# Last two images of a deformable convolution: the fine hats loaded to 32 partitions and copied on, and half of the first sums on another engine

## The chip, the cores and the metric

The kernel runs on one core of one Trainium2 chip. The metric is the device time of one execution in microseconds (us), over repeated executions. All data is float32.

## The reference, cut to what matters

Two layers are computed, one after the other, on 32 images of 128 channels and 32 x 32 pixels. Layer 0 is a sequence model (an encoder, a causal convolution of 64 taps per feature, a gated matmul, a layer norm, a decoder). Layer 1 is a deformable depthwise convolution of 8 x 8 taps, and the change lies there. For each tap `t` it reads the normalised image at a shifted position, by bilinear interpolation:

```
px = gx + koff_x[t] + off_x[t];   py = gy + koff_y[t] + off_y[t]
ix = px * W/(W-1) - 0.5;          iy = py * H/(H-1) - 0.5
s  = bilinear(image, iy, ix)      # zero outside
acc += s * weight[:, t]
out = x + gelu((acc - bn_mean) * inv + bn_beta)
```

The offsets of a tap are shared by all 128 channels, so `s` is a matrix product: a window of pixels (128 of them) by channels, against the interpolation weights of these pixels for each output pixel. The weight of a pixel at column `c`, row `r` is `hat(ix - c) * hat(iy - r)` with `hat(d) = max(0, 1 - |d|)`.

## The kernel before

`main_block` runs both layers in one stream. `first_part(b)` is the gated matmul, norm and decoder of image `b` in layer 0, and `second_part(b)` is the deformable convolution of image `b`. `run_along` interleaves the two by counting costs, `first_part(b + 2)` beside `second_part(b)`, so that the order of instructions on each engine is fixed when the kernel is built. For the last two images, 30 and 31, no `first_part` is left and `second_part` runs alone. While image 30 is worked on, the steps of `prepare(31)` are put in at given places: norm, offsets, and the hats of image 31.

The hats of an image lie in DRAM: `hats[0]` has 8 rows (the x hats, for 8 columns of a window) and `hats[1]` has 16 rows (the y hats, for its 16 rows). ScalarE makes them in `hat` (two instructions on 128 x 624 values) and stores them on its own DMA queue.

`second_part` goes over 17 packs of output columns, and in each over 4 pieces of two tap rows; so an image has 68 pieces, numbered `k` through all images. A full piece has 16 slots (output columns with one tap column each) of 2 x 32 values. For a piece:

- `load_hat(k, 0)` loads `s` (shown as `ds`) in 128 partitions: 16 copies of the 8 x hats. `load_hat(k, 1)` loads `hy` (`dhy`), each of the 16 y hats 8 times. A full piece has 512 KB of each. A pack at the left or right edge has several runs of slots and issues a DMA for each run. The loads go out on the queue of SyncE (SP). `s` has 5 buffers (`SB`) and `hy` 4 (`HB`): the load of `s` for piece `k + 5` is issued after the work of piece `k`.
- `weights(k)` (L989) multiplies `s` by `hy` on VectorE, two pieces ahead, just after the first product of the piece at hand; then it issues the load of `hy` four pieces further on.
- Three matmuls (L1032), one for each window of rows, multiply the window of pixels (`xw`, shown as `dxw`) by parts of `s` into PSUM (`dps`, 4 buffers). VectorE multiplies each result by the tap's weight into `prod` (`dp`, L1035, 3 buffers).
- GpSimd adds the two tap rows of `prod` (L1044), the first sum, and then adds the sum to `acc` (`dacc`, L1049), once for each output column of the pack.

At the end of an image GpSimd scales `acc` (L1055), ScalarE applies the gelu (L1059), VectorE adds the input (L1060), and the result is stored.

Other names: `spread` stores the positions of the taps to DRAM in 16 DMAs of 8 partitions each (`rel_d<-drel`), `gather` reads them back as `dr` (L888), `turn` transposes the image on PE and copies it to SBUF on ScalarE (`dtr`, L923), and `windows` loads `xw` (L1003). In `encode`, for layer 0, `u` (512 KB) is loaded for each image.

Of the kernel before, what the change touches and what calls it, by code (L numbers as in the profile page):

```python
# [15 lines left out]
B, C, H, W = 32, 128, 32, 32  # L16
# [430 lines left out]
NCOL = PIECES * NPIECE  # L447
# [13 lines left out]
def span_of(u):  # L461

    j0, j1 = max(0, 7 - u), min(7, NU - 1 - u) + 1
    return j0, j1 - j0


def rows_of(piece):

    a, b = 15 - KY2 * piece, 23 - KY2 * piece
    return (0, a), (a, b - a), (b, H - b)  # L470
# [30 lines left out]
def main_block(nc, tc, const, ins, x, u_d, y_d, x1_d, out, offmax):  # L501
# [15 lines left out]

    T = 512
    YB = 11
    SB, HB = 5, 4  # L520
    ctx = ExitStack()
    with ctx:

        def pool(name, bufs, space=None):
            kw = {} if space is None else {"space": space}
            return ctx.enter_context(tc.tile_pool(name=name, bufs=bufs, **kw))
# [3 lines left out]
        ppool = pool("mbp", 3)  # L530
        ypool = pool("mby", YB)
        tpool = pool("mbt", 5)
# [68 lines left out]
        for i in range(2):  # L601
            t = dram1.tile([2, NCOL], F32, tag=f"rel_d{i}", name=f"rel_d{i}")
            flat = t.rearrange("a (p l) -> (a p) l", p=P // 2)
            n = 2 * NCOL // P
# [5 lines left out]
        def at(t, offset, ap):  # L610
            return bass.AP(tensor=t.tensor, offset=t.offset + offset, ap=ap)
# [6 lines left out]
        def load(n, chunks):  # L618

            if n >= len(tiles):  # L620
                return
            b, hf = tiles[n]
            cols = slice(hf * T, hf * T + T)
            if n not in loaded:
                u = two.tile([P, T], F32, tag="gu", name=f"gu_{b}_{hf}")
                nc.sync.dma_start(u, u_d[b, :, cols])
                loaded[n] = u, []
            src = y_d[:, b].rearrange("d j l -> d (j l)")[:, cols]
            for k in chunks:
                y = ypool.tile([P, T], F32, tag="gy", name=f"gy_{b}_{hf}_{k}")  # L630
                nc.sync.dma_start(y, src[k * P : (k + 1) * P])
                loaded[n][1].append(y)
# [63 lines left out]
        def first_part(b, last=False):  # L696
            for hf in range(2):
# [5 lines left out]
                for m in range(KD):  # L703
# [13 lines left out]
                    if m == 1:  # L717
                        load(n + 1, range(YB - KD))
                        dec = pdec.tile([P, T], F32, tag="dec", name=f"gpo_{b}_{hf}")
# [9 lines left out]
                    for k in range(KD):  # L729
# [3 lines left out]
                        )  # L733
                        if m == KD - 1 and k < 2 * KD - YB:
                            load(n + 1, [YB - KD + k])
                        yield MM
# [210 lines left out]
        pieces = [(b, n, i) for b in range(B) for n in range(NP) for i in range(PIECES)]  # L947
        s_of, hy_of, xw_of = {}, {}, {}

        def slots_of(n):  # L950
            return sum(span_of(u)[1] for u in PACKS[n][1])

        def runs_of(n):

            runs, slot = [], 0
            for u in PACKS[n][1]:
                j0, nj = span_of(u)
                first = u * 8 + j0
                if runs and first == runs[-1][0] + runs[-1][2]:
                    runs[-1][2] += nj  # L960
                else:
                    runs.append([first, slot, nj])
                slot += nj
            return runs

        def load_hat(k, a):

            if k >= len(pieces):
                return
            b, n, i = pieces[k]  # L970
            hats = images[b][1]
            if a == 0:
                t = s_of[k] = spool.tile([P, 16, KY2, H], F32, tag="s", name=f"ds_{k}")
            else:
                t = hy_of[k] = hypool.tile([P, 16, KY2, H], F32, tag="hy", name=f"dhy_{k}")
            for first, slot, m in runs_of(n):
                dims = [[[0, 16], [NCOL, 8]], [[NCOL, 16], [0, 8]]][a]
                nc.sync.dma_start(
                    t[:, slot : slot + m],
                    at(hats[a], i * NPIECE + first * SLOT, [*dims, [1, m * SLOT]]),  # L980
                )

        def weights(k):

            if k >= len(pieces):
                return
            m = slots_of(pieces[k][1])
            s, hy = s_of[k], hy_of.pop(k)
            nc.vector.tensor_mul(s[:, :m], s[:, :m], hy[:, :m])  # L989
            load_hat(k + HB, 1)  # L990

        def windows(b, n):

            if n == NP:
                b, n = b + 1, 0
            x0 = PACKS[n][0]
            if b == B or (n > 0 and PACKS[n - 1][0] == x0):
                return
            t = xw_of[b, x0] = three.tile(
                [P, len(YWINDOWS), C], F32, tag="xw", name=f"dxw_{b}_{x0}"  # L1000
            )
            for j, y0 in enumerate(YWINDOWS):
                nc.sync.dma_start(  # L1003
                    t[:, j, :],
                    at(images[b][0], (y0 * W + x0) * C, [[W * C, 16], [C, 8], [1, C]]),
                )

        def second_part(b, steps):


            steps = sorted([*steps, *ending], key=lambda e: e[0])
            ending.clear()
            acc = one.tile([P, W, H], F32, tag="acc", name=f"dacc_{b}")
            nc.gpsimd.memset(acc, 0.0)
            for n in range(NP):
                x0, us = PACKS[n]
                m = slots_of(n)
                xw = xw_of[b, x0]
                windows(b, n + 1)
                for i in range(PIECES):  # L1020
                    k = (b * NP + n) * PIECES + i
                    s = s_of.pop(k)
                    w = wk[:, table_of[n] : table_of[n] + m, KY2 * i : KY2 * (i + 1)]
                    prod = ppool.tile([P, 16, KY2, H], F32, tag="prod", name=f"dp_{k}")
                    for j, (y0, ny) in enumerate(rows_of(i)):
                        while steps and steps[0][0] <= 3 * (PIECES * n + i) + j:
                            steps.pop(0)[1]()
                        ps = psam.tile([P, 512], F32, tag="sam", name=f"dps_{k}_{j}")
                        ps = ps[:, : m * KY2 * ny].rearrange(
                            "p (s k y) -> p s k y", s=m, k=KY2  # L1030
                        )
                        nc.tensor.matmul(  # L1032
                            ps, xw[:, j, :], s[:, :m, :, y0 : y0 + ny], start=True, stop=True
                        )
                        nc.vector.tensor_mul(  # L1035
                            prod[:, :m, :, y0 : y0 + ny],
                            ps,
                            w[:, :, :, None].to_broadcast([P, m, KY2, ny]),
                        )
                        if j == 0:  # L1040
                            weights(k + 2)
                        yield measure(m * KY2 * ny)
                    load_hat(k + SB, 0)
                    nc.gpsimd.tensor_add(prod[:, :m, 0], prod[:, :m, 0], prod[:, :m, 1])  # L1044
                    slot = 0
                    for u in us:
                        j0, nj = span_of(u)
                        to = acc[:, u - 7 + j0 : u - 7 + j0 + nj]
                        nc.gpsimd.tensor_add(to, to, prod[:, slot : slot + nj, 0])  # L1049
                        slot += nj  # L1050

            o = two.tile([P, L], F32, tag="img", name=f"do_{b}")
            xr = two.tile([P, L], F32, tag="img", name=f"dxr_{b}")
            nc.sync.dma_start(xr, x1_d[b])
            nc.gpsimd.tensor_scalar(  # L1055
                o.rearrange("p (h w) -> p w h", w=W), acc, bn_mean, bn_inv,
                op0=ALU.subtract, op1=ALU.mult,
            )
            ending.append((6, lambda: nc.scalar.activation(o, o, AF.Gelu, bias=bn_beta)))  # L1059
            ending.append((11, lambda: nc.vector.tensor_add(o, o, xr)))  # L1060
            ending.append((14, lambda: nc.scalar.dma_start(out[b], o)))

        ending = []
        def measure(columns):

            return columns + 40.0
# [24 lines left out]
        for b in range(B):  # L1091
            steps = prepare(b + 1) if b + 1 < B else []
            if b + 2 < B:
                run_along(
                    (first_part(b + 2, last=(b + 2 == B - 1)), FIRST),
                    (second_part(b, steps), SECOND),
                )
            else:
                run_along((second_part(b, steps), SECOND))
# [152 lines left out]
```

## Time and profile before

| | |
|---|---|
| time, median of 3 runs | 14067.17 us (14044.14 to 14073.55) |
| the profiled execution: its own time | 14059.14 us |
| its span, first to last instruction | 14057.0 us |
| PE busy (share of the span) | 13268.5 us (94%) |
| VectorE busy | 8827.7 us (63%) |
| GpSimd busy | 9113.7 us (65%) |
| ScalarE busy | 3215.1 us (23%) |
| moved by DMA | 3172.55 MB, mean 226 GB/s |

The engines are PE (matmul) and PEld (weight load) of TensorE, DVE (VectorE), ACT (ScalarE), POOL (GpSimd) and SP (SyncE). Shares of busy time are means over stages with different limits, so a change in one stage is read from stretches of the time line. Lines such as L989 are lines of the kernel before. A group of instructions is shown with its output and input by name and shape, its count, its busy time and mean, and the idle time of its engine just before it with what ended that.

### The profile page before, as it was taken

Reading aid. Unit: us, or ns where it says so; the run is one execution under the profiler, and the core shown is the slowest. Engines: PE = TensorE matmul, PEld = TensorE weight load, DVE = VectorE, ACT = ScalarE, POOL = GpSimd, SP = SyncE. Lnnn points to the kernel's source line nnn. Section 1 sums busy time; section 2 is a strip of 40 time slices with the busy share of each in tenths; the row PEclk is TensorE's granted clock in tenths of the full one; section 3 lists DMA queues with packets and bytes.
Section 4 is the critical chain, followed back from the end, with each engine's and each line's share of the span. In section 5 each row is a group of like instructions: output and inputs, shape, how many; then the busy total and the mean of one; then the engine's idle time right before and its main releaser. Section 6 shows DMA issues by size and latency. Waiting matters only on the chain.

```text
span 14057.0 us, 134776 instructions
## 1 busy us (share of the span) xinstructions
PE 13268.5 (94%) x40482; PEld 7317.0 (52%) x40482; DVE 8827.7 (63%) x12555; ACT 3215.1 (23%) x5422; POOL 9113.7 (65%) x9158
## 2 busy tenths in 40 slices
PE   5888889999999999999999999999999999999965
PEld 4777744555555555555555555555555555555532
DVE  6666614666666666666666666666666666666655
ACT  3445412222222222222222121222222222222210
POOL 1334413777777777777777777777777777777767
PEclk9999999999999999999999999999999999999977
DMA  6777724888888888888888888888888888889888
GB/s 224 232 232 230 222 79 126 239 237 235 233 231 232 231 233 238 236 235 230 231 232 229 229 229 230 229 234 237 239 236 233 230 233 231 233 236 237 233 228 227
DMA packets 1741840, 3172.55 MB, mean 226 GB/s; under 512 B 311218, under 2 KB 1030450, under 8 KB 1740082
## 3 DMA queue, kind: packets, MB, share of 16 engines
q1 hardware_dynamic: 1528498, 2708.63, 72.9%
q10 hardware_dynamic: 163456, 320.92, 6.4%
q0 software_dynamic: 49152, 134.28, 3.1%
q8 instruction: 329, 5.39, 0.2%
q14 instruction: 405, 3.32, 0.1%
HBM read 2697.07 MB, written 466.06 MB: 225 GB/s over the span
## 4 chain that ended last, share of the span: by engine, by line
PE 75%; DMA 10%; DVE 7%; POOL 3%; issue 2%; ACT 2%; SPq 1%; DVEq 0%; ACTq 0%; POOLq 0%
PE gpg L707 22%; PE gpv L730 21%; PE dps L1032 21%; DMA ds<-dhat 6%; PE psz L227 4%; PE gph L746 3%; PE gpo L639 3%; DVE dco L839 2%; DVE ds L989 2%; POOL y_d L296 1%; DMA y_d<-yo 1%; PE psy L266 1%; DVE dp L1035 1%; ACT t L280 1%; DMA dhy<-dhat 1%
## 5 line engine op out<-in xcount | busy, mean ns | idle before, releaser
L1032 PE MATMUL dps<-ds,dxw 128*128 128x256 f32 (+18 forms) x13056 | 4737.7, 450 | 308.0 <-DVE dp L1035 305.7
L1035 DVE TENSOR_TENSOR dp<-dps,k_weight_slots 128x256 f32<-128x256 f32 (+17 forms) x6528 | 3061.5, 485 | 2868.8 <-PE dps L1032 2578.2
L1049 POOL TENSOR_TENSOR dacc<-dacc,dp 128x256 f32<-128x256 f32 (+3 forms) x4736 | 4224.6, 892 | 371.4
L1044 POOL TENSOR_TENSOR dp<-dp 128x512 f32<-128x512 f32 (+3 forms) x2176 | 2858.6, 1314 | 2159.3 <-DVE dp L1035 2140.9
L1032 PEld LDWEIGHTS dps<-ds,dxw 128*128 128x128 f32 x13056 | 2478.6, 193 | 3330.7 <-issue 2510.7
L707 PE MATMUL gpg<-gy,g_w_glu 128*128 128x512 f32 x8192 | 3986.6, 593 | 19.1 <-DMA gy<-y_d 14.3
L730 PE MATMUL gpv<-gy,g_w_glu 128*128 128x512 f32 x8192 | 3975.3, 592 | 0.0
L989 DVE TENSOR_TENSOR ds<-ds,dhy 128x1024 f32<-128x1024 f32 (+3 forms) x2176 | 3158.0, 1451 | 1242.4 <-DMA ds<-dhat 1165.3
L707 PEld LDWEIGHTS gpg<-gy,g_w_glu 128*128 128x128 f32 x8192 | 1544.6, 190 | 1235.2 <-issue 974.2
L730 PEld LDWEIGHTS gpv<-gy,g_w_glu 128*128 128x128 f32 x8192 | 1548.9, 189 | 1158.2 <-issue 915.2
L767 ACT ACTIVATE gq<-gr 128x512 f32<-128x512 f32 x448 | 282.3, 630 | 5050.9 <-DVE gr L759 4725.9
L768 POOL TENSOR_TENSOR gs<-gs,gq 128x512 f32<-128x512 f32 x448 | 599.1, 1337 | 1267.2 <-ACT gq L767 1267.1
L266 PE MATMUL psy<-toe,z 128*128 128x192 f32 x4096 | 790.2, 353 | 222.9 <-DVE t L277 214.8
L266 PEld LDWEIGHTS psy<-toe,z 128*128 128x128 f32 x4096 | 735.5, 207 | 273.4 <-issue 211.1
L714 ACT ACTIVATE gs<-gpg,k_b_glu 128x512 f32<-128x512 f32 x512 | 351.8, 687 | 2151.3 <-PE gpg L707 2078.9
L903 ACT ACTIVATE dh<-dr,k_minus 128x624 f32<-128x624 f32 x768 | 620.5, 808 | 933.4 <-DMA dr<-rel_d 493.5
L296 POOL DMA_DIRECT2D y_d<-yo x1024 | 589.1, 583 | 351.8 <-ACT yo L290 324.2
L738 DVE SCALAR_TENSOR_TENSOR gs<-gpv,k_b_glu,gs 128x512 f32<-128x512 f32 x512 | 379.9, 742 | 413.8 <-PE gpv L730 413.8
L641 POOL TENSOR_TENSOR gs<-gs,gr 128x512 f32<-128x512 f32 x448 | 635.3, 1418 | 0.0
L904 ACT ACTIVATE dh<-dh,one 128x624 f32<-128x624 f32 x768 | 626.3, 815 | 25.0
L227 PE MATMUL psz<-w_enc,u 128*128 128x128 f32 x4096 | 584.5, 288 | 24.0 <-DVE z L234 9.1
L275 POOL MEMSET t<- 32x256 f32 x256 | 72.4, 322 | 776.0 <-ACT yo L290 775.1
(164 smaller groups left out, 6620.3 us busy)
## 6 DMA issues: line engine op xcount, KB each, us to landing
dhy<-dhat SPq DMA_DIRECT2D x1536, 512.0 KB
ds<-dhat SPq DMA_DIRECT2D x1536, 512.0 KB
dhat<-dh ACTq DMA_DIRECT2D x768, 312.0 KB
u<-u_d SPq DMA_DIRECT2D x256, 512.0 KB
y_d<-yo POOLq DMA_DIRECT2D x1024, 128.0 KB, 3.7
gy<-y_d SPq DMA_DIRECT2D x512, 256.0 KB
toe<-kp_d SPq DMA_DIRECT2D x128, 768.0 KB
dxw<-dvt_d SPq DMA_DIRECT2D x1248, 64.0 KB
```

Of the source, the lines that this page charges most:

```text
L227: nc.tensor.matmul(ps[:, j, :], u[:, (NB * g + j) * P : (NB * g + j + 1) * P], w_enc[:, k * P : (k + 1) * P], start=True, stop=True,)
L266: nc.tensor.matmul(ps[:, c // 2, c % 2, :], rows[i][:, g * CG + c0 + c, :], toe[:, c0 + c, :], start=True, stop=True,)
L296: nc.gpsimd.dma_start(y_d[d0 : d0 + CG, :, i * NB + j, :].rearrange("d b l -> b d l"), yo[i][j * B : (j + 1) * B],)
L641: nc.gpsimd.tensor_add(sums[0], sums[0], r)
L707: nc.tensor.matmul(gate, w_glu[:, k, D + m * P : D + m * P + P], ys[k], start=(k == 0), stop=(k == KD - 1),)
L730: nc.tensor.matmul(val, w_glu[:, k, m * P : m * P + P], ys[k], start=(k == 0), stop=(k == KD - 1),)
L904: nc.scalar.activation(t, t, AF.Relu, scale=-1.0, bias=const["one"])
L989: nc.vector.tensor_mul(s[:, :m], s[:, :m], hy[:, :m])
L1032: nc.tensor.matmul(ps, xw[:, j, :], s[:, :m, :, y0 : y0 + ny], start=True, stop=True)
L1035: nc.vector.tensor_mul(prod[:, :m, :, y0 : y0 + ny], ps, w[:, :, :, None].to_broadcast([P, m, KY2, ny]),)
L1044: nc.gpsimd.tensor_add(prod[:, :m, 0], prod[:, :m, 0], prod[:, :m, 1])
L1049: nc.gpsimd.tensor_add(to, to, prod[:, slot : slot + nj, 0])
```

## The change

For images 30 and 31 (`b >= ALONE`) the load of `s` brings 4 copies of the 8 x hats to 32 partitions, a quarter of the bytes. `spread_fine` then makes the other 96 partitions on ScalarE: partitions 0 to 31 are copied to 32 to 63, and 0 to 63 to 64 to 127. It is called one piece ahead of `weights`, just after it in program order. Of the first sums of these images, those of pieces with odd `i`, two of four, go to VectorE in place of GpSimd. The loads of `hy`, the matmuls and the number of DMAs are as before, and nothing changes for images 0 to 29 but three calls of `spread_fine` in the last three pieces of image 29.

```diff
+    ALONE = B - 2
...
+            rows = 4 if a == 0 and b >= ALONE else 16
             for first, slot, m in runs_of(n):
-                dims = [[[0, 16], [NCOL, 8]], [[NCOL, 16], [0, 8]]][a]
+                dims = [[[0, rows], [NCOL, 8]], [[NCOL, rows], [0, 8]]][a]
                 nc.sync.dma_start(
-                    t[:, slot : slot + m],
+                    t[: rows * 8, slot : slot + m],
                     at(hats[a], i * NPIECE + first * SLOT, [*dims, [1, m * SLOT]]),
                 )
+
+        def spread_fine(k):
+
+            if k >= len(pieces) or pieces[k][0] < ALONE:
+                return
+            m = slots_of(pieces[k][1])
+            for n in (32, 64):
+                nc.scalar.copy(s_of[k][n : 2 * n, :m], s_of[k][:n, :m])
...
                         if j == 0:
                             weights(k + 2)
+                            spread_fine(k + 3)
                         yield measure(m * KY2 * ny)
                     load_hat(k + SB, 0)
-                    nc.gpsimd.tensor_add(prod[:, :m, 0], prod[:, :m, 0], prod[:, :m, 1])
+                    adder = nc.vector if b >= ALONE and i % 2 else nc.gpsimd
+                    adder.tensor_add(prod[:, :m, 0], prod[:, :m, 0], prod[:, :m, 1])
```

## The prediction

> **What bounds the kernel now.** I read the span in equal slices first: PE is 90% busy or more in nearly all of it and falls to 60% only at the end. The timeline of GpSimd puts the clear of `acc` for image 30 at 13434 us and for image 31 at 13770 us, and the sum of image 31 ends at 14045 us. So the change acts on a tail of some 610 us, 136 pieces (2 images x 17 packs x 4). Busy time by stretch (us, PE, PEld, DVE, ACT, POOL, granted clock, DMA share, GB/s):
>
> ```profile
> 13000.00:13400.00 400.00, 398.37 (x1097) 205.12 (x1096) 261.24 (x358) 77.66 (x104) 287.00 (x268) 1.00 0.83 226
> ...
> 13825.00:13865.00 40.00, 23.50 (x59) 11.81 (x59) 25.62 (x39) 0.00 (x0) 33.02 (x31) 0.88 1.04 267
> ...
> 13945.00:13985.00 40.00, 23.20 (x54) 11.20 (x54) 23.87 (x39) 0.00 (x0) 30.78 (x27) 0.83 1.04 253
> ```
>
> Before the tail PE is full and DMA isn't. In it PE is 58% busy, ScalarE idle, GpSimd 80%, and the DMA engines are full (1.04). Groups of instructions from 13600 to 14000 us (busy, mean ns | idle before, releaser):
>
> ```profile
> L1049 POOL TENSOR_TENSOR dacc<-dacc,dp 128x256 f32<-128x256 f32 x142 | 139.1, 980 | 11.1
> ...
> L989 DVE TENSOR_TENSOR ds<-ds,dhy 128x1024 f32<-128x1024 f32 x70 | 97.0, 1386 | 136.9 <-DMA ds<-dhat 136.9
> L1044 POOL TENSOR_TENSOR dp<-dp 128x512 f32<-128x512 f32 x69 | 88.3, 1280 | 80.3 <-DVE dp L1035 80.3
> ```
>
> VectorE waits 137 us of 400 for the load of `ds`; PE waits for VectorE, and so does GpSimd. The chain of waits from 13800 us (start, length):
>
> ```profile
> 13800.56 10.59 DMA ds<-dhat
> 13811.15 0.02 issue
> 13811.17 0.04 DVE ds L989
> 13811.21 1.26 issue
> 13812.47 0.42 DVE dp L1035
> 13812.89 0.04 issue
> 13812.94 0.24 PE dps L1032
> 13813.18 9.66 DMA ds<-dhat
> ```
>
> A turn is 12.62 us: a load of `ds` is issued when PE has read the buffer, lands 10.6 us later, and is multiplied three pieces on. That is 4.21 us a piece. Weights counted from 13797 to 14000 us say the same: 46 full pieces and 4 half ones in 203 us, 4.23 us. A full piece loads 512 KB of `ds`, 512 KB of `dhy` and on average 48 KB of `dxw`; 68.6 kB on each of 16 engines in 4.23 us is 16.2 GB/s each. The queue is full, so the landing time is mostly queueing.
>
> [...] Stretches: image 31, 13900 to 13950 us; the encoder's loads of `u`, 205 to 245 us; and 13505 to 13545 us, with 16 stores of 8 partitions each.
>
> ```profile
> DMA packets 4100, 12.18 MB, mean 244 GB/s; under 512 B 455, under 2 KB 1228, under 8 KB 4097
> ...
> DMA packets 2498, 9.11 MB, mean 228 GB/s; under 512 B 284, under 2 KB 284, under 8 KB 2494
> q1 hardware_dynamic: 2494, 9.05, 73.7%
> ...
> DMA packets 7576, 6.74 MB, mean 168 GB/s; under 512 B 4499, under 2 KB 6285, under 8 KB 7574
> ```
>
> In the first, 2872 packets of 4 KB are 22.4 hat loads and 773 of 512 B are 6 loads of `dxw`; 455 completions over 28.4 DMAs is 16.0 each. In the last, the stores have 16 x 256 packets of 128 B, which leaves 403 completions; 17 other DMAs by their data take 272, and 131 over 16 stores is 8.2 each. Eight on the outer dim, eight engines. The changed load has 4. [...] two `dacc` sums take 1.52 us alone and 2.39 us when L989 runs beside them.
>
> **The change part by part.**
> *Bytes.* `ds` falls from 512 to 128 KB a piece. But source `[0, 4], [NCOL, 8]` puts those on 4 engines: 32 KB each, what each engine carries of it now. Engines 0 to 3 still have 32 + 32 + 3 KB, 68.6 kB a piece; the other twelve have half. So the bytes saved don't by themselves shorten the load; it does so only if those four go faster once the others ask for less. Bounds: 16.2 GB/s, nothing gained, 4.23 us; and the encoder's loads of 4 KB rows, 9.05 MB in 16 x 40 us x 73.7% = 19.2 GB/s, giving 3.57 us. During the tail, bursts above 380 GB/s occur where hat stores on ScalarE's queue join, so neither fabric nor engine is at its end[...]. Total demand falls to 5/8; I take 18.4 GB/s, three quarters of the way: 3.73 us, 0.50 us less. Over 2 x 48 full-piece equivalents: **-48 us** (0 to -63).
> *Other engines at 3.73 us.* VectorE: 1.39 (L989) + 0.65 + 0.42 + 0.45 (L1035) + half an add = 3.3 us. GpSimd: 1.28 + 2 x 0.98 = 3.2 us, or 2.0 on odd pieces. PE: 29.93 us for 11 pieces, 2.7. SP: two issues of 0.55 us. None is over 3.73, though VectorE is near.
> *Two ScalarE copies a piece, on the path.* The nearest row, `dv<-dx` 128x1024, is 1.06 us[...]. Two, the second after the first, 2.3 us with the waits: 313 us of an idle engine, but it lengthens each turn of the ring. [...] The queue gives way, 0 here.
> *ScalarE's order in image 30.* Spreads now stand between the hats of image 31 (24 x 2 x 0.815 us), which wait for `dr` (21.8 us now) and for their own stores (54.1 us). A full ScalarE piece is 2.3 + 1.15 us, still under 3.73; but a spread behind the first hat waits for `dr`, which lands some 11 us after its issue at piece 23: about 4 us once. PE's small matmuls of the group norm and the copies of `dtr` wait behind spreads, 1 us each. Together **+8 us** (0 to +20). Image 29's last three pieces have three such pairs beside first_part; 2.3 us each, slack of four PSUM buffers, taken at 0.
> *68 first sums moved.* GpSimd loses 68 x 1.28 = 87 us; VectorE gains 68 adds of 128x512. [...] the trace's L989 with 512 elements has 0.68 at least and 1.09 mean beside GpSimd. It delays the next piece's first product by that, inside VectorE's 1.5 us wait. At the end GpSimd does four pieces at 3.07 us after PE is done; two lose 1.12 us: **-2 us**. At each image's start GpSimd is late after L1055 and the clear: two odd pieces of the first four shed 1.1 us, **-5 us** over both. Pieces of 4 or 2 runs keep their 8 or 4 issues of 0.62 us on SP: 0.
> Sum: -48 + 8 - 2 - 5 = **-47 us** on the profiled execution's 14059.1 us (span 14057.0). The median of the three runs is 8 us above that; from 14067.2 it gives 14020.
>
> **The rivals.**
> *B, no gain (0.20).* Engines 0 to 3 carry the same bytes at the same 16.2 GB/s; the period stays 4.23 us and only +8 - 7 is left: 14068. For it: hat packets move at the same 250 to 260 GB/s whatever their size. Against: the encoder's and the bursts above.
> *C, slower (0.20).* ScalarE's spread becomes a serial stage and the queue doesn't give way. If `ds` on engines 0 to 3 still lands after 10.6 us, a turn is 10.6 + 2.3 + 2.0 = 14.9 us, 4.97 us a piece: +0.76 x 96 = +73, 14141. It decides from a landing of 8.3 us; at 9.2 us it costs 28 us. For it: DMA waits end last, and a queue behind four engines may not shorten. Against: in a ring limited by service, time added elsewhere comes off the queue.
> *D, the load spreads over all 16 engines (0.06).* 705 kB a piece at 260 GB/s is 2.7 us, and VectorE at 3.3 plus stalls, 3.45, sets the pace: -0.78 x 96 - 7 + 8, -74: 13993. The count of 8.2 above speaks against it.
>
> **How the numbers follow.** About 0.2%, 28 us, is what a measurement of this kernel can tell from no change. A, the forecast, has 0.54: its own range is 13990 to 14045; 0.49 of it is faster, 0.05 within. B: 0.17 same, 0.01 faster, 0.02 slower. C: 0.18 slower, 0.02 same. D: faster. Faster 0.56, same 0.24, slower 0.20. The range reaches from D with full speed on top (13970) into the lower half of C (14105).
>
> **What the profile would show.** Completions per `ds` load: 4 for A, B and C, 16 for D. DMA share in the tail: about 0.6 to 0.75 for A, B and C. The wait of L989: for ScalarE rather than for DMA. Weights per 50 us in image 31: 13 for A, 11.5 for B, 10 for C, over 14 for D. ScalarE copies near 1.05 us, VectorE's add 0.7 to 1.1 us, `dacc` 0.98 us or less. I am wrong on A if the four engines' period stays over 4.1 us, or if another engine than DMA sets it.

## The result and the profile after

The changed kernel takes 13994.6 us (median of 4, 13974.8 to 13997.3) against 14058.7 us of the kernel before in the same comparison (14044.1 to 14073.6): a ratio of 0.9951, 95% interval 0.9934 to 0.9969. That is 64 us less; 47 were forecast. The total alone would fit rival D (13993 us) better than the forecast (14020); which of the two it was is read from the profile. The changed profile was taken at 13997.3 us (span 13995.3). Lines have moved by 10 to 12: L989 is now L999, L1035 is L1045, the first sum L1044 is L1056 and the column sums L1049 are L1061; the spread is L991.

Busy time by stretch in image 31 of the changed kernel (us, PE, PEld, DVE, ACT, POOL, granted clock, DMA share, GB/s):

```profile
13770.00:13940.00 170.00, 113.42 (x291) 54.22 (x289) 157.21 (x217) 96.55 (x97) 132.93 (x116) 0.91 0.68 189
...
13865.00:13915.00 50.00, 32.37 (x86) 15.04 (x87) 48.59 (x65) 29.48 (x29) 41.52 (x36) 0.96 0.72 201
```

The DMA share is down from 1.04 to 0.68 and VectorE up to 157 us of 170, 92%; in the second stretch it is 97%. The groups of 13770 to 13940 us:

```profile
L1061 POOL TENSOR_TENSOR dacc<-dacc,dp 128x256 f32<-128x256 f32 x92 | 103.7, 1127 | 26.0 <-DVE dp L1056 20.7
L999 DVE TENSOR_TENSOR ds<-ds,dhy 128x1024 f32<-128x1024 f32 x44 | 72.7, 1651 | 12.0 <-ACT ds L991 11.8
L991 ACT COPY ds<-ds 64x1024 f32<-64x1024 f32 x44 | 45.9, 1044 | 1.4
L991 ACT COPY ds<-ds 32x1024 f32<-32x1024 f32 x43 | 44.9, 1044 | 62.1 <-DMA ds<-dhat 59.8 <-PE dps L1042 2.3
...
L1056 DVE TENSOR_TENSOR dp<-dp 128x512 f32<-128x512 f32 x23 | 23.7, 1032 | 0.8
```

VectorE's wait before the product of hats is 12 us of 170, where it was 137 of 400, and it is for ScalarE. The 44 full pieces and 4 half ones make 3.70 us a piece (4.23 before), with a half piece counted as half. The product itself has grown from 1.39 to 1.65 us. The chain of waits from 13795 us:

```profile
13795.71 6.05 DMA ds<-dhat
...
13801.84 1.05 ACT ds L991
...
13802.92 1.05 ACT ds L991
...
13804.00 1.78 DVE ds L999
13805.78 0.35 DVE dp L1045
...
13806.17 3.09 PE dps L1042 x6
...
13810.01 6.28 DMA ds<-dhat
```

A load now lands in 6.1 to 6.3 us (9.7 to 10.6 before); the two copies stand between it and the product. The packets of 13765 to 13815 us:

```profile
DMA packets 4152, 9.68 MB, mean 194 GB/s; under 512 B 460, under 2 KB 1983, under 8 KB 4150
```

2167 packets of 4 KB, at 128 + 32 a piece, are 13.5 pieces; 1523 of 512 B are 11.9 loads of `dxw`. Of the 460 packets under 512 B, taken as completions, one for each engine that carries a DMA, 16 x 25.4 belong to those and to `dhy`, and the 54 left over 13.5 loads of `ds` are 4.0 each. The packet records agree: from 13770 to 13940 us exactly four packets were in flight for 14.1% of the time, more than any other count but 16 (15.5%); in the kernel before, from 13797 to 13997 us, 16 or more were in flight for 97%. The changed load runs on four engines, so the rival with 16 is out.

**The measure used below.** From GpSimd's clear of `acc` for image 30 to that for image 31, and from there to the last scaling, each profile gives the length of the two images. The time ahead of the tail, where nothing differs but the layout, varied from 13427 to 13449 us between kernels, so these lengths resolve more than the totals; the changed kernel profiled twice gave 546.7 and 544.1 us. Ratios are to the kernel before, with their 95% interval.

| kernel | image 30, us | image 31, us | both, us | ratio |
|---|---|---|---|---|
| before | 335.8 | 270.8 | 606.6 | 1 |
| the change | 304.1 | 242.6 | 546.7 | 0.9951 (0.9934 to 0.9969) |
| the change again | 303.5 | 240.6 | 544.1 | 0.9964 (0.9951 to 0.9978) |
| load alone, sums as before | 302.0 | 243.8 | 545.8 | 0.9952 (0.9938 to 0.9965) |
| sums alone | 337.8 | 275.5 | 613.3 | 1.0006 (0.9997 to 1.0014) |
| 64 partitions, one copy | 317.5 | 252.7 | 570.2 | 0.9968 (0.9956 to 0.9980) |
| four loads of 8 partitions | 337.8 | 251.7 | 589.5 | 0.9989 (0.9981 to 0.9997) |
| all bytes on four engines | 581.0 | 509.3 | 1090.3 | one run, 14558.6 us |
| one sum in four on VectorE | 302.9 | 238.2 | 541.1 | 0.9956 (0.9942 to 0.9969) |
| load on 16 engines | 294.5 | 234.5 | 529.0 | 0.9955 (0.9941 to 0.9968) |
| both of these | 297.4 | 230.9 | 528.3 | 0.9951 (0.9937 to 0.9965) |
| fewer column sums | 296.7 | 232.5 | 529.2 | one run, 13979.8 us |
| both, and stores by ScalarE | 293.3 | 231.2 | 524.5 | 0.9949 (0.9936 to 0.9963) |

### The profile page after: what moved, and what is told of

The parts are those of the page before. It is cut to its first block, busy times and chain, and to the rows that moved or that the text cites. A ratio compares the mean times of both kernels' runs of the same rounds, so it can differ in the third digit from the quotient of the medians.

```text
span 13995.3 us, 135396 instructions
## 1 busy us (share of the span) xinstructions
PE 13264.8 (95%) x40482; PEld 7312.4 (52%) x40482; DVE 8898.8 (64%) x12623; ACT 3484.1 (25%) x5694; POOL 9051.0 (65%) x9090
## 3 DMA queue, kind: packets, MB, share of 16 engines
q14 instruction: 409, 3.35, 0.1%
## 4 chain that ended last, share of the span: by engine, by line
PE 76%; DMA 8%; DVE 8%; ACT 3%; POOL 2%; issue 2%; SPq 1%; ACTq 0%; DVEq 0%; POOLq 0%
PE gpg L708 23%; PE gpv L731 21%; PE dps L1042 21%; DMA ds<-dhat 5%; PE psz L227 4%; PE gph L747 3%; PE gpo L640 3%; DVE ds L999 2%; DVE dco L840 2%; POOL y_d L296 2%; DMA y_d<-yo 1%; PE psy L266 1%; DVE dp L1045 1%; ACT t L280 1%; DVE drel L857 1%
## 5 line engine op out<-in xcount | busy, mean ns | idle before, releaser
L1045 DVE TENSOR_TENSOR dp<-dps,k_weight_slots 128x256 f32<-128x256 f32 (+17 forms) x6528 | 3059.5, 483 | 2853.2 <-PE dps L1042 2570.6
L1061 POOL TENSOR_TENSOR dacc<-dacc,dp 128x256 f32<-128x256 f32 (+3 forms) x4736 | 4239.7, 895 | 457.7 <-DVE dp L1056 89.3
L1056 POOL TENSOR_TENSOR dp<-dp 128x512 f32<-128x512 f32 (+3 forms) x2108 | 2779.6, 1319 | 2066.6 <-DVE dp L1045 2048.4
L999 DVE TENSOR_TENSOR ds<-ds,dhy 128x1024 f32<-128x1024 f32 (+3 forms) x2176 | 3175.1, 1459 | 1118.7 <-DMA ds<-dhat 971.2
```

The lines of the kernel that those rows point to most:

```text
L1045: nc.vector.tensor_mul(prod[:, :m, :, y0 : y0 + ny], ps, w[:, :, :, None].to_broadcast([P, m, KY2, ny]),)
L1056: adder.tensor_add(prod[:, :m, 0], prod[:, :m, 0], prod[:, :m, 1])
```

## The experiments

### The two halves of the change apart

```diff
-                    adder = nc.vector if b >= ALONE and i % 2 else nc.gpsimd
+                    adder = nc.gpsimd
```

> The load to 32 partitions and the ScalarE copies as in the change, all first sums on GpSimd. Theory (the load is the gain; VectorE, at 92% to 97% busy in image 31 after the change, is what now binds beside the four DMA engines): most of the gain stays, 40 to 70 us under the kernel before; VectorE has an add of 0.96 us less on every other piece, so a period near 3.6 to 3.8 us, with GpSimd at 3.7 us a piece the next bound. Rival (the moved sums are the gain, GpSimd was the hidden limit): 0 to 15 us under the kernel before, period over 4.1 us.

The load alone has the whole gain: 545.8 us for the two images, as the change. What differs is which engine is full. Busy time by stretch in this kernel's image 31, and its waits there (us, times, longest):

```profile
13778.00:13948.00 170.00, 110.45 (x287) 52.48 (x285) 133.35 (x190) 96.94 (x98) 159.16 (x138) 0.92 0.67 187
```

```profile
DVE dp L1045 <- POOL dacc L1061: 21.6, 33, 1.0
...
DVE ds L999 <- ACT ds L991: 12.8, 16, 2.0
```

VectorE is at 78%, GpSimd at 94%, and the products wait for `prod` buffers that GpSimd still holds. The moved sums exchange one full engine for another.

The other half alone puts back `rows = 16` and leaves out the call of `spread_fine`:

```diff
-            rows = 4 if a == 0 and b >= ALONE else 16
+            rows = 16
...
-                            spread_fine(k + 3)
```

> Only the every other first sum on VectorE for the last two images; the loads as before on 128 partitions, no ScalarE copies. Theory: GpSimd wasn't the bound, so 0 to 10 us faster, from the edges and the last four pieces alone; L989's wait for DMA stays near 137 us of 400. Rival (the moved sums are the gain): 40 us or more faster.

1.0006, no gain. The wait for the load in the kernel before, from 13797 to 13997 us, and the waits of this one from 13812 to 13997 us:

```profile
DVE ds L989 <- DMA ds<-dhat: 72.2, 45, 3.0
...
DVE ds L999 <- DMA ds<-dhat: 56.0, 39, 3.3
POOL dacc L1060 <- DVE dp L1055: 49.4, 22, 4.2
```

VectorE still waits for the load for 30% of the time (36% before), and GpSimd now waits for the sums that VectorE makes: work was taken from an engine that bound nothing. The 0 to 10 us expected at the edges did not show either.

### How many engines carry the load

```diff
-            rows = 4 if a == 0 and b >= ALONE else 16
+            rows = 8 if a == 0 and b >= ALONE else 16
...
-            for n in (32, 64):
+            for n in (64,):
```

> 8 copies to 64 partitions in place of 4 to 32, one ScalarE copy of 64 partitions in place of two. Eight engines then carry 64 KB of hats a piece instead of four, the other eight 32 KB; the path has one ScalarE copy (1.05 us) less. Theory (a loaded engine speeds up because the others ask for less): period between before and after, 3.8 to 3.9 us, 10 to 25 us slower than the change. Rival 1 (the ring's latency with its two copies binds): faster than the change by 10 us or more. Rival 2 (VectorE alone binds): the same as the change within 8 us.

24 us more for the two images than the change, and 3.83 us a piece (45 full and 4 half pieces in 180 us). Two things differ here, one copy less on the path and twice as many loaded engines, and the second outweighs the first: the copies are not the larger cost, but that they cost nothing isn't shown. The wait is DMA again, in image 31 from 13780 to 13960 us:

```profile
ACT ds L991 <- DMA ds<-dhat: 112.9, 42, 4.5
...
DVE ds L999 <- ACT ds L991: 30.5, 26, 3.2
```

Next, the kernel before with the same 512 KB, cut so that four engines carry them:

```diff
+                if a == 0 and b >= B - 2:
+                    for c in range(4):
+                        nc.sync.dma_start(
+                            t[32 * c : 32 * c + 32, slot : slot + m],
+                            at(hats[a], ..., [[0, 4], [NCOL, 8], [1, m * SLOT]]))
+                    continue
```

> The kernel before with the load of s for the last two images made as four DMAs of 32 partitions, each with 4 copies as the outer count: the same 512 KB, by four engines in place of sixteen, no ScalarE copies. A loaded engine has 128 + 32 + 3 KB = 167 kB a piece, the other twelve 35 kB. Theory (four engines carry it, at about 19 GB/s once the others are mostly idle): 8.8 us a piece, some 400 us slower. [...] Rival (the count of engines doesn't follow the outer count): within 40 us of the kernel before, for the extra issues on SP alone.

14558.6 us, 499 us slower than the kernel before beside it, at half the DMA share (47% from 14160 to 14260 us). The groups from 14160 to 14460 us:

```profile
L999 DVE TENSOR_TENSOR ds<-ds,dhy 128x1024 f32<-128x1024 f32 x38 | 46.5, 1225 | 190.7 <-DMA ds<-dhat 180.0 <-DMA dhy<-dhat 10.7
...
L999 DVE TENSOR_TENSOR ds<-ds,dhy 128x512 f32<-128x512 f32 x4 | 3.9, 975 | 8.2 <-DMA ds<-dhat 6.7 <-issue 1.5
```

40 piece equivalents in 300 us are 7.5 us each. A loaded engine has 163 KB (166.9 kB) a piece: 22.3 GB/s, above the 19 of the expectation. That gives a row of rates, each from the bytes of a loaded engine and the measured period: 16.2 GB/s with all 16 engines loaded, 17.9 with eight loaded and eight at half (64 partitions), 18.5 with four loaded and twelve at half (the change, where VectorE binds as well), 22.3 with four loaded and twelve at a fifth. In these four kernels a loaded engine ran faster the less the others asked for, and that was the step on which the forecast rested. The change's rate is a lower bound, since its engines also wait for VectorE.

The packet records of the traces show how. With all bytes on four engines, a packet of 4 KB took 165 ns on average while at most four packets were in flight, and 253 ns while 15 or more were; in the change 171 and 221 ns. In the kernel before nearly all its packets had 15 or more in flight, and took 261 ns. So a loaded engine wasn't fast all along in these runs: it was slow while all 16 ran and fast once the others had done their share. An estimate from 16.2 GB/s while all run and 24.8 GB/s (4 KB in 165 ns) after that, with 35.8 kB a piece on each of the other twelve, gives 3.5 us a piece for the change and 7.5 for this run; the full packs of image 31 took 3.63 and 7.33. For 64 partitions it also gives 3.5, where 3.82 were measured: the eight engines together didn't reach the rate of the four. Why packets took longer when all ran is not shown by these runs.

### Taking the four engines away

First, four DMAs of 8 partitions in place of one, where a piece is one run:

```diff
+                if rows == 4 and len(runs_of(n)) == 1:
+                    for c in range(rows):
+                        nc.sync.dma_start(
+                            t[c * 8 : c * 8 + 8, slot : slot + m],
+                            at(hats[a], ..., [[NCOL, 8], [1, m * SLOT]]))
+                    continue
```

> As the change, but the load of one piece (where it is one run of slots) is issued as four DMAs of 8 partitions, whose outer count is 8: eight engines carry 16 KB each of it, 51 KB with the rest, in place of 67 KB on four. SP issues 5 DMAs a piece, about 2.8 us. Theory (four engines and VectorE bind about equally): landing 1 us sooner, ScalarE's wait for DMA halved, but a gain of 0 to 15 us only since VectorE is at 92%. Rival (the four engines alone bind): 25 us or more faster.

A miss: 43 us worse than the change over the two images, 34 of them in image 30. SP's own waits from 13427 to 13765 us:

```profile
SPq L982 <- DMA dhy<-dhat: 29.6, 20, 2.1
...
SPq L982 <- DMA dhat<-dh: 21.9, 9, 4.0
...
SPq L990 <- DMA dhat<-dh: 12.4, 5, 3.8
```

With five DMAs a piece, SP waits for earlier ones to land before it issues the next, for stores on ScalarE's queue too; in the change its waits for `dhat` stores in image 30 are 6.0 us. The expectation counted SP's issue time (2.8 us a piece) and not these waits. Why an issue waits there was not taken further.

Then one DMA on 16 engines: the x hats of the last two images are stored four times, so that 32 plain rows can be read.

```diff
-                            [(8, 16)[a], NCOL], F32, ...
+                            [(32, 16)[a], NCOL], F32, ...
...
+                    if a == 0 and b >= ALONE:
+                        nc.scalar.dma_start(
+                            at(st["h0"], k * NCOL, [[HSUB, P], [8 * NCOL, 4], [1, HSUB]]),
+                            t[:, None, :].to_broadcast([P, 4, HSUB]))
+                        return
...
+                if rows == 4:
+                    dims = [[NCOL, 32]]
```

> As the change, but the x hats of the last two images are stored four times (one store DMA each, four times the bytes, 7.5 MB more per image), so that the load to 32 partitions is 32 plain rows, one DMA on 16 engines with 8 KB each. An engine then has 43 KB a piece, 2.3 us. Theory (four engines and VectorE bind about equally): ScalarE's wait for DMA falls by half or more, landing 4 us or less, period 3.45 to 3.6 us, 5 to 20 us faster than the change if the added stores cost image 30 little. Rival (the four engines alone bind): 30 us or more faster. Rival 2 (VectorE alone): the same within 5 us.

The two images take 17.7 us less than in the change (529.0 against 546.7), where two profiles of the change differ by 2.6 us. From 13830 to 13880 us its loads have 15.6 completions each. So the four engines were a part of the bound. Busy time in its image 31, from 13770 us, then ScalarE's wait for the load in the change (170 us) and here (160 us):

```profile
13770.00:13930.00 160.00, 107.21 (x276) 51.29 (x275) 152.63 (x208) 92.31 (x92) 126.75 (x112) 0.91 0.81 192
...
ACT ds L991 <- DMA ds<-dhat: 67.4, 42, 3.5
...
ACT ds L999 <- DMA ds<-dhat: 58.3, 42, 4.0
```

VectorE is at 95%. In one stretch of its chain, from 13800 to 13830 us, loads land in 4.3 to 4.9 us, yet ScalarE still waits 58 us of 160 for them, where it was 67 of 170 in the change and I had expected half: a load is issued only when PE has freed the buffer, and that follows VectorE. Its packets of 4 KB take 272 ns on average, 233 in the change: the same bytes spread over 16 engines land sooner, though each packet takes longer. The total time, 13997.7 us, does not resolve the 18 us; the ratio has the change's interval.

### The sums' share

```diff
-                    adder = nc.vector if b >= ALONE and i % 2 else nc.gpsimd
+                    adder = nc.vector if b >= ALONE and i == 1 else nc.gpsimd
```

> As the change, with one first sum of four on VectorE (i = 1) in place of two. Theory (VectorE at 92% with two, GpSimd at 94% with none, so the period follows the fuller of the two): both near 87%, 5 to 15 us faster than the change, unless the four DMA engines (67 KB a piece, 3.57 us at 19.2 GB/s) hold it: then within 5 us of the change. Rival (the sums' place doesn't matter, DMA alone binds): the same within 5 us and landing times as in the change.

541.1 us, 3 to 6 us under the change's two profiles, at the edge of what these resolve. VectorE falls to 82% and GpSimd rises to 90%:

```profile
13775.00:13945.00 170.00, 111.79 (x291) 55.07 (x292) 140.22 (x207) 97.88 (x98) 152.51 (x130) 0.91 0.68 191
```

> The two before this together: 16 engines for the load, one first sum of four on VectorE. Theory: with DMA off the path, VectorE and GpSimd near 90% each set it: 3.35 to 3.5 us a piece, 15 to 35 us faster than the change. Rival (something else, PE's clock or the order of work, holds 3.6 us): the same within 8 us.

528.3 us, 18 under the change and within 1 us of the 16-engine load alone; in total 13988.6 us. Busy time in image 31:

```profile
13770.00:13930.00 160.00, 104.49 (x283) 52.49 (x282) 140.81 (x202) 94.76 (x95) 147.53 (x124) 0.92 0.83 196
```

The period is 3.56 us (43 full and 4 half pieces in 160 us) with VectorE at 88% and GpSimd at 92%: the 3.35 to 3.5 us of the theory were not reached.

### Why VectorE's product grew

In the changed kernel's time line (start, length):

```profile
13810.14 1.26 POOL L1056 TENSOR_TENSOR dp<-dp 128x512 f32<-128x512 f32 x1 [0.20 <-DVE dp L1045]
13810.48 2.00 DVE L999 TENSOR_TENSOR ds<-ds,dhy 128x1024 f32<-128x1024 f32 x1
...
13811.47 2.39 POOL L1061 TENSOR_TENSOR dacc<-dacc,dp 128x256 f32<-128x256 f32 x2
```

The product takes 1.23 us alone. Here it starts 0.34 us after a GpSimd sum of 1.26 us and takes 2.00: nearly as if it began when that ended, 13811.40 + 1.23 = 13812.63 against 13812.48. To test it, part of GpSimd's column sums is left out:

```diff
+                        if b < ALONE or u == us[0]:
                             nc.gpsimd.tensor_add(to, to, prod[:, slot : slot + nj, 0])
```

> As the change, but for the last two images only the first output column of each pack is added to acc; the sums into the other columns are left out, some half of GpSimd's work there (0.76 us alone, 1.1 us as measured, a full piece). Theory (VectorE's L999 is stretched from 1.24 us to 1.65 us by GpSimd beside it, and with that VectorE, the four DMA engines and GpSimd are bounds of nearly one size): L999 falls to 1.25 to 1.4 us and VectorE from 92% to 80% or so; the four engines' 67 KB then hold a period of 3.1 to 3.4 us (22 to 20 GB/s), 30 to 45 us less for the two images. Rival (L999 is long for another reason): it stays over 1.55 us and the time within 10 us of the change. Rival 2 (DMA alone was the bound): L999 falls, the period stays at 3.6 to 3.7 us.

Groups from 13770 to 13930 us:

```profile
L999 DVE TENSOR_TENSOR ds<-ds,dhy 128x1024 f32<-128x1024 f32 x42 | 66.0, 1572 | 15.3 <-ACT ds L991 15.1
...
L1056 DVE TENSOR_TENSOR dp<-dp 128x512 f32<-128x512 f32 x22 | 15.2, 692 | 0.8
```

The moved sum falls from 1.03 to 0.69 us, but the product only from 1.65 to 1.57, and the two images take 17.5 us less, not 30 to 45. My expectation of 1.25 to 1.4 failed: with GpSimd at 49%, 37 of the 42 products still start while a GpSimd instruction is under way (40 of 44 in the change). Where GpSimd has long been done, with all bytes on four engines, the product takes 1.225 us. The traces show how the two share the time. In each of these 44 and 42 products the length is 1.225 us plus what is left of the GpSimd instruction under way at the start, less 0.15 us, to within 0.02 us; one that starts later adds nothing. It is the GpSimd instruction that is longer then: a column sum of 128x256 takes 0.72 us alone, but one that starts within a product ends 0.58 us after it, and takes 1.59 us (median; 45 of 92 in the stretch of the change). So the stretch goes with the instruction that is under way, not with GpSimd's share. How much time it costs in the change stays open.

### A version faster than the change

To the last combination, the 16 stores of `rel_d` for image 31 are issued by ScalarE, spread over seven steps:

```diff
-                        nc.sync.dma_start(
+                        (nc.sync if only is None else nc.scalar).dma_start(
...
+            if b == B - 1:
+                stores = [(61 + 7 * n / 16, spread(n // 8, n % 8)) for n in range(16)]
```

> The 16-engine load with one sum in four on VectorE, and besides the 16 stores of rel_d for image 31 issued by ScalarE, spread over steps 61 to 68, in place of SP in a block of 12.8 us, behind which the hat loads wait in the change (VectorE idle for 11.4 us at 13535 us). Theory: 7 to 11 us less in image 30 than the kernel without it (297 us from clear to clear), 25 to 40 us faster than the change in all. Rival (the wait moves to ScalarE's copies behind the stores): within 3 us.

> The change itself, on the chip and in the rounds of the run before it, for a direct comparison: 13975 to 14000 us, 0.994 to 0.996 of the kernel before; image 30 302 to 306 us from clear to clear, image 31 241 to 244 us to its last GpSimd instruction's start.

13979.4 us (13967.3 to 13990.7) beside 13998.3 us of the change (13995.0 to 14005.3): 19 us less, with ranges that do not overlap, and 0.9949 of the kernel before; less than the 25 to 40 us expected. (The change itself came to 0.9964, just over the 0.994 to 0.996 expected.) Image 30 is 4.1 us shorter than without the moved stores, of the 7 to 11 expected: VectorE's longest wait for the spread was 9.8 us without this and is 7.2 us with it, ScalarE now standing behind `down` and its own stores. Beside the 2.6 us between two profiles of one kernel, 4.1 us is hardly resolved, and the rival (within 3 us) isn't excluded. By the lengths of the two images most of the 19 us belongs to the 16-engine load.

## Why the prediction was right, step by step

- *What bounds it.* The load of `ds`: shown by the two halves apart, the load with the whole gain and the sums with none.
- *The load runs on 4 engines.* Shown by 4.0 completions a load, by four packets in flight, and by 499 us lost when all bytes went that way. Which four of the 16 they are, no trace shows: "engines 0 to 3" in the forecast is a name for them. (The line from 13900 us has 2869 packets of 4 KB, 4097 less 1228, and not 2872; the 16.0 completions stay.)
- *The loaded engines speed up.* 18.4 GB/s and 3.73 us were taken between 16.2 and 19.2; 18.5 GB/s and 3.70 us came out, and the row of rates shows the direction. The upper bound was too low: 22.3 GB/s was seen. The agreement is partly luck. One of the listed signs of being wrong, that another engine than DMA sets the period, is half met: VectorE was at 92%, and image 31 came down by 8 us with the load on 16 engines and by 10 us with fewer column sums, so the four engines did not set it alone.
- *Size of this term.* -48 us; the load alone has 60.8 us less for the two images, its ScalarE costs in image 30 included. This is the term that was too small. It took 0.50 us off each of 96 full pieces. By the starts of the product of hats, the twelve full packs went from 4.20 to 3.63 us a piece in image 31 and from 5.13 to 4.53 in image 30, 0.57 and 0.60 us less, 57 of the 60 us by which the change shortens both images. The count was right: the packs at the edges gave about 1 us. The gain of a piece was set too low. Image 30, whose pieces were slower before, was taken to gain no more than image 31, and gained a little more.
- *ScalarE's order, +8 us.* Not seen as a sum: the load alone gained 33.8 us in image 30 and 27.0 in image 31. Of its parts, the wait of a spread behind a hat that waits for `dr` did not come: in image 30 of the change ScalarE waits neither for `dr` (21.8 us before) nor for its own stores (54.1 us), and its copies wait 5.8 us in all for hats. The longest wait of VectorE in the tail, 11.4 us behind the 16 stores of `rel_d`, was 9.1 us before: the two copies of 2.1 us were added to it, once.
- *The moved sums, -7 us.* The last four pieces gave their 1.5 us (11.7 from 13.2 us, with -2 forecast), but nothing is left in the sum: 1.0006 alone, and none beside the load (546.7 and 544.1 us with the moved sums, 545.8 without). The term should have been 0.
- *VectorE.* Named as near the limit at 3.3 us; it takes 3.42 us a piece, since the product went from 1.39 to 1.65 us. Of the signs listed, `dacc` at 0.98 us or less was wrong (1.13): 45 of 92 column sums start within a product in the stretch of the change, 30 of 92 in that of the kernel before.
- *The ring.* Landings of 6.1 to 6.3 us were seen on the chain, well under the 8.3 us from which the slower rival decides. One copy less with twice the loaded engines made the kernel slower, so the copies were not the larger cost.

That the two terms +8 and -7, neither of which came, nearly cancel is luck; the error is the mis-sized first term, 48 us against the 61 us of the load alone.

## What to carry to other kernels

Divide a DMA's bytes by the engines that carry it, not by 16: here the load with an outermost count of 4 brought 128 KB in place of 512 and left 68.6 kB a piece on the four engines that it used, and 4.0 completions per load in the packet counts told the number. When a full resource is relieved, the next bound is read from its busy time and from how its own instructions stretch: VectorE went from 63% to 92%. Moving work between two engines that were both next in line gained nothing here.

## What the runs showed of the hardware

On rows of 4 KB that are read 4 to 16 times over, an engine moved 16.2 GB/s when all 16 were loaded (the kernel before) and 22.3 GB/s when four were (all bytes on four engines); in the latter run a packet took 165 ns with at most four in flight and 253 ns with 15 or more. VectorE's product of two SBUF tiles (1.23 us alone, 1.65 us on average in the change) and GpSimd's sums (a column sum 0.72 us alone, 1.59 us when it started within a product) took turns: whichever started later finished as if it had waited for the other but for 0.15 us. Issuing the load of a full piece took SP 0.65 us on 4 engines and 32 partitions in the change, 0.55 us on 16 and 128 in the kernel before: a quarter of the bytes was issued no faster. A ScalarE copy of 1024 elements took 1.044 us on 32 and on 64 partitions in the change.
